# Memory of the scans reused in the tail: eight weight buffers, combination weights kept, the last two combinations side by side

## The chip, the core and the metric

The kernel runs on one core of a Trainium2 chip. Times are device microseconds of one launch, from one core. The time before is the median of three runs, 5513.0 us (5512.04 to 5520.48). The profile is one more execution, recorded by the hardware profiler.

## The reference

The input `x` holds 16 sequences of 512 rows and 256 columns. A bidirectional selective-scan layer is added to it and normalised; then follows a soft mixture of experts, with 16 experts of 64 slots each, which is added and normalised again. The last part is what the change touches:

```python
x = _layernorm(x + _L0_attn_ref(x, ...))            # scans, forward and backward
# mixture of experts, xn = layernorm(x) * g + b
logits = einsum('bnd,esd->bnes', xn, se)            # 1024 slots for each row
dispatch = softmax(logits, axis=1)                  # over the 512 rows
combine = softmax(logits.reshape(b, n, -1), -1)     # over the 1024 slots
slots = einsum('bnd,bnes->besd', xn, dispatch)
gate = gelu(einsum('besd,edf->besf', slots, Wg) + bg)
up = einsum('besd,edf->besf', slots, Wu) + bu
eout = einsum('besf,efo->beso', gate * up, Wd) + bd
y = einsum('bns,bso->bno', combine, eout)
out = _layernorm(x + y)
```

All data is float32. The experts' weights are 48 blocks of 512 KB (`Wg`, `Wu`, `Wd` for each of 16 experts).

## The kernel before

**The loop.** `seq_layers` goes through the 16 sequences. For each one it runs four scan parts (`scan_part`, two directions by two pairs of channel blocks). Beside the scans, in small pieces, it runs three streams of other work, each a list of Python generators in a `Side` object: `prep` (projections for the next scan parts), `front` (`finish`, which ends the first layer for the sequence before, and `dispatch`, which makes the slots) and `back` (`experts` and `combine` for older sequences). A generator yields how many PSUM banks its next piece needs, or `HOLD` when the results of a piece are to be taken out later. The order in which pieces are asked for sets their priority; a scheduler then places each engine's instructions, and `late` marks those that must keep their place. On each engine the instructions run strictly in the order that results from it, and so do the DMA issues of SP.

**Experts.** Sequences are taken in twos: `experts(g, 0, 8)` handles sequences 2g and 2g+1 together, 128 rows for each expert. It goes through eight pairs of experts. For a pair, PE multiplies the slots `st` with both `Wg` (L709, into `pg`), ScalarE applies gelu (L728, L731, into `ht`); then for each expert PE makes `pu` with `Wu` (L666), VectorE multiplies it into `ht` (L678), PE multiplies `ht` with `Wd` (L694, into `peo`), VectorE adds the bias `bd` (L659, into `eo`) and SP stores `eo` to `e_dram` (L660). `prefetch` (L632) keeps three weight tiles loaded or on the way, in three buffers of 512 KB. `st`, `bd` and `eo` have one buffer each: the next `bd` is loaded (L691) when `eo` has read the last one, the next `st` (L645) when the last `pu` of the pair is done.

**Combine.** `combine(b)` loads the 1024 rows of expert output of its sequence (`ceo`, L754), x1 (`cx`, L759), and for each of four blocks of 128 rows a tile of x2 (L763). For each block PE makes the logits (`cl`, L785, four matmuls of 512 columns, eight records in the profile), VectorE the maxima (L797 to L799), ScalarE exp (`cm`, L802), PE eight transposes (`ctp`, L809), ScalarE the copies (`ct`, L814), and PE eight matmuls with the expert outputs (`cpo`, L820, 16 records). The outputs carry a column of ones (L751), so `cpo` holds the sum of the weights as well: VectorE takes its reciprocal (L773) and adds the scaled result to x1 (L774). When all four blocks are done the rows are normalised (L49, L50 on VectorE; L51, L52, L488, L489 on POOL; L494 on ScalarE) and written out in one DMA (L834). `ceo` and `cx1` have one buffer, so the next combination's loads wait for this one.

**Dispatch.** For each of eight blocks of 128 slots: logits `pl` (L571), maximum (L576), exp with its sum (L579), reciprocal, scaling (L581), transposes `pd` (L585), a copy into `dis` (L590); after each second block the slots `pq` (L600), their copy `sl` (L610) and the store to `s_dram` (L619). `et`, `dis` and `sl` have one buffer.

**The tail.** After the last scan part the PSUM banks of the scans are given to a second pool (`tail`), and the rest runs without scans beside it: what is left of `combine(13)`, then `finish` and `dispatch` of sequence 15, then `experts(7, 0, 8)`, `combine(14)` and `combine(15)` in one list, one after the other (L875 to L884).

Of the kernel before, what the change touches and what calls it, by code (L numbers as in the profile page):

```python
# [9 lines left out]
F32 = mybir.dt.float32  # L10
BF16 = mybir.dt.bfloat16
AF = mybir.ActivationFunctionType
ALU = mybir.AluOpType
# [42 lines left out]
def seq_layers(tc, ident, neghalf, a, out):  # L56
# [21 lines left out]
    with ExitStack() as ctx:  # L78
# [7 lines left out]
        p2 = ctx.enter_context(tc.tile_pool(name="m_p2", bufs=2))  # L86
        p3 = ctx.enter_context(tc.tile_pool(name="m_p3", bufs=3))
        dram = ctx.enter_context(tc.tile_pool(name="m_dram", bufs=3, space=DRAM))
        ps = ctx.enter_context(tc.tile_pool(name="m_ps", bufs=3, space=PSUM))
# [5 lines left out]
        BANKS = 3  # L95
        tail = []
        count = [0]
# [162 lines left out]
        def prep_pair(b, r, p, v, gate=None):  # L260
# [18 lines left out]
            for c, q, pz in pzs:  # L279
                dts[c] = dt = p2.tile([P, L], F32, tag="dt", name=f"dt_{q}", bufs=4)  # L280
                if len(dts) == 1 and gate is None:
                    act = nc.scalar.activation(dt, pz, AF.Softplus)
                    late(act)
                else:
                    with tc.high_priority():
                        nc.scalar.activation(dt, pz, AF.Softplus)
            yield HOLD
            for c, q, pz in pzs:
                dt = dts[c]

                rr = p2.tile([P, L], F32, tag="rr", name=f"rr_{q}", bufs=4)
# [8 lines left out]
                du = p2.tile([P, L], F32, tag="du", name=f"du_{q}", bufs=4)  # L300
                nc.gpsimd.tensor_tensor(du, dt, v["u"][:, c, :], ALU.mult)
                v[c] = (dt, rr, du)
# [35 lines left out]
        def scan_part(b, r, p, v, accs, done, then):  # L338
# [4 lines left out]
            for n in range(0, NS, 2):  # L343
                q = f"{b}_{r}_{p}_{n}"

                bs = p3.tile([P, 2, L], F32, tag="bs", name=f"bs_{q}")
                cs = p3.tile([P, 2, L], F32, tag="cs", name=f"cs_{q}", bufs=2)
                for t, rows in ((bs, v["bc"][0, n : n + 2, :]), (cs, v["bc"][1, n : n + 2, :])):
                    nc.sync.dma_start(t, rows.unsqueeze(0).to_broadcast([P, 2, L]))
                for c in (2 * p, 2 * p + 1):  # L350
                    dt, rr, du = v[c]
                    db = p3.tile([P, 2, L], F32, tag="db", name=f"db_{q}_{c}")
                    nc.gpsimd.tensor_tensor(db, du.unsqueeze(1).to_broadcast([P, 2, L]), bs, ALU.mult)  # L353
                    hg = p3.tile([P, 2, L], F32, tag="hg", name=f"hg_{q}_{c}", bufs=4)
                    for j in range(2):
                        s = slice(n + j, n + j + 1)
                        h = ps_h.tile([P, L], F32, tag="h", name=f"h_{q}_{c}_{j}")
                        nc.scalar.activation(h, dt, AF.Exp, scale=w["A"][:, c, s])  # L358
                        th = p3.tile([P, L], F32, tag="th", name=f"th_{q}_{c}_{j}")
# [204 lines left out]
        def dispatch(b, xn, x2T):  # L564

            for sc in range(NSC):
# [9 lines left out]
                late(nc.vector.reduce_max(nm, pl, AX.X, negate=True))  # L576
                et = p1.tile([P, L], F32, tag="et", name=f"et_{i}")
                sm = p3.tile([P, 1], F32, tag="sm", name=f"sm_{i}")
# [42 lines left out]
        def experts(g, lo, hi):  # L621
# [10 lines left out]
            def prefetch():  # L632
                while len(got) < min(used[0] + 3, len(needs)):
                    key, e = needs[len(got)]
                    t = p2.tile([P, 4 * DM], F32, tag="W", name=f"{key}_{g}_{e}", bufs=3)
                    src = a[key][e]
# [109 lines left out]

        def combine(b):


            eo = p1.tile([P, NSC, DM + 1], F32, tag="ceo", name=f"ceo_{b}")  # L750
            nc.gpsimd.memset(eo[:, :, DM : DM + 1], 1.0)  # L751
            own = e_dram[:, b * SL : (b + 1) * SL, :]
            for j in range(2):
# [3 lines left out]
                )  # L757
            x1 = p1.tile([P, NL, DM], F32, tag="cx1", name=f"cx1_{b}")
            nc.sync.dma_start(x1, x1_dram[b].rearrange("(c p) d -> p c d", p=P))  # L759

            def load_x2(lc):
                t = p2.tile([P, NM, P], F32, tag="cx2", name=f"cx2_{b}_{lc}")
                nc.sync.dma_start(t, x2_dram[b, :, :, lc * P : (lc + 1) * P].rearrange("k p l -> p k l"))  # L763
                return t

            x2 = load_x2(0)
            yield 0
            prev = []

            def take_in():  # L770
                lc, po = prev.pop()
                sm = p3.tile([P, 1], F32, tag="csm", name=f"csm_{b}_{lc}")
                late(nc.vector.reciprocal(sm, po[:, DM : DM + 1]))  # L773
                nc.vector.scalar_tensor_tensor(  # L774
                    x1[:, lc, :], po[:, :DM], sm, x1[:, lc, :], ALU.mult, ALU.add
                )

            for lc in range(NL):
                i = f"{b}_{lc}"
                yield 2  # L780
                cls = []
                for h in range(2):
                    cl = bank(f"cl_{i}_{h}")
                    for k in range(NM):
                        nc.tensor.matmul(  # L785
                            cl,
                            x2[:, k, :],
                            seT[:, k, h * 512 : (h + 1) * 512],
                            start=(k == 0),
                            stop=(k == NM - 1),  # L790
                        )
                    cls.append(cl)
                if lc + 1 < NL:
                    x2 = load_x2(lc + 1)
                yield HOLD
                nm = p3.tile([P, 3], F32, tag="cnm", name=f"cnm_{i}")
                late(nc.vector.reduce_max(nm[:, 0:1], cls[0], AX.X))  # L797
                nc.vector.reduce_max(nm[:, 1:2], cls[1], AX.X)
                nc.vector.reduce_max(nm[:, 2:3], nm[:, 0:2], AX.X, negate=True)  # L799
                cms = [p3.tile([P, 512], F32, tag="cm", name=f"cm_{i}_{h}") for h in range(2)]  # L800
                for cm, cl in zip(cms, cls):
                    nc.scalar.activation(cm, cl, AF.Exp, bias=nm[:, 2:3])  # L802
                yield 2
                pts = []
                for h in range(NSC // 4):
                    pt = bank(f"ctp_{i}_{h}")
                    for j in range(4):
                        s = slice(j * P, (j + 1) * P)
                        nc.tensor.transpose(pt[:, s], cms[h][:, s], ident)  # L809
                    pts.append(pt)  # L810
                yield HOLD
                cts = [p3.tile([P, 512], F32, tag="cm", name=f"ct_{i}_{h}") for h in range(2)]
                for h, pt in enumerate(pts):
                    ins = nc.scalar.copy(cts[h], pt)  # L814
                    if h == 0:
                        late(ins)
                yield 1
                po = bank(f"cpo_{i}")
                for sc in range(NSC):
# [6 lines left out]
                    )  # L826
                prev.append((lc, po))
                yield HOLD
                take_in()
            mv, rs = row_stats(nc, p2, x1, neghalf, "c1")  # L830
            sh = shifts(mv, rs, "c1")
            yield 0
            scaled(x1, x1, sh, rs)
            nc.scalar.dma_start(out[b].rearrange("(c p) d -> p c d", p=P), x1)  # L834

# [40 lines left out]
        scan_psum.close()  # L876
        tail.append(ctx.enter_context(tc.tile_pool(name="t_ps", bufs=5, space=PSUM)))
        BANKS = 8
        back.drain()
        front.drain()  # L880
        g = nb // 2 - 1
        for gen in (experts(g, 0, 8), combine(2 * g), combine(2 * g + 1)):
            back.add(1, gen)
        back.drain()  # L884

# [45 lines left out]
```

## Time and profile before

| what | value |
|---|---|
| median of three runs | 5513.0 us |
| the profiled execution | 5517.41 us |
| its span, first to last instruction | 5515.6 us |
| mean granted TensorE clock | 0.861 |
| busy: PE, VectorE, ScalarE, POOL | 4004.2, 4522.2, 4097.3, 4998.6 us |
| last scan transpose on PE | ends at 5189.9 us |
| last dispatch matmul (`pq`) of sequence 15 | ends at 5298.1 us |
| last `eo` of the experts | ends at 5414.4 us |
| first `cpo` of `combine(14)` | starts at 5423.2 us |

Busy time is the time in which an engine ran an instruction. The slices of the page divide the span into 40 equal parts, with one digit for the busy tenths of each. A row of the stretches gives the same by engine for a chosen window. A wait names the engine and line that waited, what ended the wait, and the total, the number and the longest. The chain of work is followed back from the last instruction, at each step to what released it.

### The profile page before, as it was taken

Reading aid. Unit: us, or ns where it says so; the run is one execution under the profiler, and the core shown is the slowest. Engines: PE = TensorE matmul, PEld = TensorE weight load, DVE = VectorE, ACT = ScalarE, POOL = GpSimd, SP = SyncE. Lnnn points to the kernel's source line nnn. Section 1 sums busy time; section 2 is a strip of 40 time slices with the busy share of each in tenths; the row PEclk is TensorE's granted clock in tenths of the full one; section 3 lists DMA queues with packets and bytes.
Section 4 is the critical chain, followed back from the end, with each engine's and each line's share of the span. In section 5 each row is a group of like instructions: output and inputs, shape, how many; then the busy total and the mean of one; then the engine's idle time right before and its main releaser. Section 6 shows DMA issues by size and latency. Waiting matters only on the chain.

```text
span 5515.6 us, 67752 instructions
## 1 busy us (share of the span) xinstructions
PE 4004.2 (73%) x21330; PEld 3097.9 (56%) x21330; DVE 4522.2 (82%) x6210; ACT 4097.3 (74%) x6662; POOL 4998.6 (91%) x2525
## 2 busy tenths in 40 slices
PE   4556656777777777777777777777777777877777
PEld 3434444666556655666555655566556556566565
DVE  7787878888888889889888888888898898888512
ACT  6667677778778887878878787788778788777522
POOL 6999999999999999999999999999999999989500
PEclk7667777888988989888998899989899889999998
DMA  4333333565445654465545654456544665467253
GB/s 132 112 108 126 121 117 124 167 199 188 157 138 195 203 193 140 144 207 193 172 139 173 203 191 151 147 190 203 186 144 146 203 195 172 137 212 240 83 161 96
DMA packets 493852, 897.76 MB, mean 163 GB/s; under 512 B 44307, under 2 KB 291731, under 8 KB 493493
## 3 DMA queue, kind: packets, MB, share of 16 engines
q1 hardware_dynamic: 454836, 851.48, 47.6%
q10 hardware_dynamic: 38656, 41.95, 2.2%
q8 instruction: 169, 2.77, 0.2%
q14 instruction: 191, 1.56, 0.1%
HBM read 832.47 MB, written 60.82 MB: 162 GB/s over the span
## 4 chain that ended last, share of the span: by engine, by line
DVE 34%; ACT 24%; PE 18%; issue 11%; POOL 10%; DMA 3%; SPq 0%; DVEq 0%; ACTq 0%; POOLq 0%
DVE h L364 9%; DVE h L362 9%; DVE hg L367 8%; ACT h L358 5%; ACT th L360 5%; POOL hg L368 4%; POOL db L353 4%; PE acc L317 3%; PE px L244 2%; DVE rr L299 2%; PE cl L785 2%; PE pg L709 2%; ACT L358 2%; PE cpo L820 1%; ACT ht L731 1%
## 5 line engine op out<-in xcount | busy, mean ns | idle before, releaser
L353 POOL TENSOR_TENSOR db<-du,bs 128x1024 f32<-128x1024 f32 x1024 | 2431.3, 2374 | 113.8 <-DVE h L362 48.6
L368 POOL TENSOR_TENSOR hg<-hg,cs 128x1024 f32<-128x1024 f32 x1024 | 2427.6, 2371 | 25.4 <-DVE hg L367 17.6
L367 DVE SCALAR_TENSOR_TENSOR hg<-th,h 128x512 f32<-128x512 f32 x2048 | 1352.3, 680 | 251.1 <-ACT th L360 139.9
L317 PE MATMUL acc<-ident,hg 128*128 128x128 f32 x8192 | 1214.9, 301 | 391.4 <-POOL hg L368 316.0
L317 PEld LDWEIGHTS acc<-ident,hg 128*128 128x128 f32 x8192 | 1069.2, 157 | 634.1 <-POOL hg L368 410.9
L364 DVE TENSOR_TENSOR_SCAN h<-h,db 128x512 f32<-128x512 f32 x1024 | 1227.2, 1221 | 191.0 <-ACT h L358 155.2
L362 DVE TENSOR_TENSOR_SCAN h<-h,db 128x512 f32<-128x512 f32 x1024 | 1222.8, 1221 | 180.6 <-ACT h L358 131.7
L358 ACT ACTIVATE h<-dt,A_f 128x512 f32<-128x512 f32 x1024 | 699.9, 683 | 319.2 <-DVE hg L367 316.5
L358 ACT ACTIVATE h<-dt,A_b 128x512 f32<-128x512 f32 x1024 | 700.0, 684 | 292.6 <-DVE hg L367 290.9
L360 ACT ACTIVATE th<-rr,Ah_b 128x512 f32<-128x512 f32 x1024 | 728.0, 711 | 0.3
L360 ACT ACTIVATE th<-rr,Ah_f 128x512 f32<-128x512 f32 x1024 | 726.9, 710 | 0.2
L694 PE MATMUL peo<-Wd,ht 128*128 128x256 f32 x1024 | 314.8, 461 | 190.4 <-DVE ht L678 129.4
L694 PEld LDWEIGHTS peo<-Wd,ht 128*128 128x128 f32 x1024 | 223.2, 227 | 263.1 <-DVE ht L678 143.3
L709 PE MATMUL pg<-st,Wg 128*128 128x128 f32 x2048 | 277.7, 297 | 85.5 <-ACT xb L219 40.6
L785 PE MATMUL cl<-seT,cx 128*128 128x512 f32 x512 | 279.4, 689 | 75.3 <-DVE rr L299 36.7
L709 PEld LDWEIGHTS pg<-st,Wg 128*128 128x128 f32 x2048 | 265.7, 211 | 97.2 <-ACT xb L219 42.1
L666 PE MATMUL pu<-st,Wu 128*128 128x128 f32 x2048 | 270.2, 288 | 33.3 <-ACT ht L731 11.8
L666 PEld LDWEIGHTS pu<-st,Wu 128*128 128x128 f32 x2048 | 257.5, 203 | 57.0 <-ACT ht L731 16.8
L571 PE MATMUL pl<-x2T,seT 128*128 128x512 f32 x512 | 261.1, 634 | 22.9 <-DVE xf L168 12.5
L600 PE MATMUL pq<-dis,xn 128*128 128x256 f32 x1024 | 253.8, 405 | 15.7 <-ACT dis L590 13.0
L820 PE MATMUL cpo<-ceo,ct 128*128 128x257 f32 x1024 | 249.3, 398 | 21.9 <-ACT ct L814 17.0
L751 POOL MEMSET ceo<- 128x8 f32 x16 | 2.0, 124 | 260.4 <-PE cpo L820 259.4
(146 smaller groups left out, 5356.6 us busy)
## 6 DMA issues: line engine op xcount, KB each, us to landing
bs<-bc SPq DMA_DIRECT2D x512, 512.0 KB, 4.6
cs<-bc SPq DMA_DIRECT2D x512, 512.0 KB, 3.7
Wg<-in_Wg_dram SPq DMA_DIRECT2D x128, 512.0 KB, 5.4
Wu<-in_Wu_dram SPq DMA_DIRECT2D x128, 512.0 KB, 5.7
Wd<-in_Wd_dram SPq DMA_DIRECT2D x128, 512.0 KB, 5.6
bd<-in_bd_dram SPq DMA_DIRECT2D x128, 128.0 KB, 4.7
s_dram<-sl ACTq DMA_DIRECT2D x64, 256.0 KB, 2.9
st<-s_dram SPq DMA_DIRECT2D x128, 128.0 KB, 4.3
```

Source lines behind the costliest of these rows:

```text
L317: ins = nc.tensor.matmul(accs[c][:, s], hc[:, j, s], ident, is_transpose=True, start=False, stop=(last and j == 1 and lc == NL - 1),)
L353: nc.gpsimd.tensor_tensor(db, du.unsqueeze(1).to_broadcast([P, 2, L]), bs, ALU.mult)
L358: nc.scalar.activation(h, dt, AF.Exp, scale=w["A"][:, c, s])
L360: nc.scalar.activation(th, rr, AF.Tanh, bias=LN_1E12 / 2, scale=w["Ah"][:, c, s])
L362: nc.vector.tensor_tensor_scan(h, h, db[:, j, :], 0.0, ALU.mult, ALU.add)
L364: nc.vector.tensor_tensor_scan(h[:, ::-1], h[:, ::-1], db[:, j, ::-1], 0.0, ALU.mult, ALU.add)
L367: nc.vector.scalar_tensor_tensor(hg[:, j, :], th, 1.0, h, ALU.add, ALU.mult)
L368: nc.gpsimd.tensor_tensor(hg, hg, cs, ALU.mult)
L666: nc.tensor.matmul(pu[:, fc * P : (fc + 1) * P], got["Wu", e][:, k, fc * P : (fc + 1) * P], st[:, k, :, j * SL : (j + 1) * SL], start=(k = ...
L694: nc.tensor.matmul(po[:, :DM], ht[:, fc, :], got["Wd", e][:, fc, :], start=(fc == 0), stop=(fc == NF - 1))
L709: nc.tensor.matmul(pg[:, fc * P : (fc + 1) * P], got["Wg", e][:, k, fc * P : (fc + 1) * P], st[:, k, :, j * SL : (j + 1) * SL], start=(k = ...
L785: nc.tensor.matmul(cl, x2[:, k, :], seT[:, k, h * 512 : (h + 1) * 512], start=(k == 0), stop=(k == NM - 1),)
```

## The change

The pools of the scans' SBUF tiles are put into one pool, `m_scan` (`p4`), which is closed after the last scan part. A new pool, `t_sb`, takes its memory (`wide`). While `wide` is set:

- the experts' weights have eight buffers in place of three (`AHEAD`), and `prefetch` asks for eight;
- `dispatch` has three `et` buffers in place of one;
- the weights of a combination (logits, exp, transposes, copies) are a generator of their own, `weights`, and `all_weights` runs it for the four blocks of a sequence and keeps the eight copied tiles;
- `combine` takes kept tiles if it is given them, and then does only `cpo`, the sum, the norm and a write for each block of 128 rows (128 KB each) in place of one norm and one write at the end;
- `ceo` of sequence 15 has its own buffer; both x1 tiles are in the buffers of `x`; the column of ones is set by VectorE in place of POOL.

The tail then runs two lists in turn, a piece of each: the rest of `combine(13)` and `all_weights(14)` beside `finish` and `dispatch` of sequence 15; the experts beside `all_weights(15)`; `combine(14)` beside `combine(15)`.

```diff
+        scan_room = ctx.enter_context(ExitStack())
+        p4 = scan_room.enter_context(tc.tile_pool(name="m_scan", bufs=3))
...
-                dts[c] = dt = p2.tile([P, L], F32, tag="dt", name=f"dt_{q}", bufs=4)
+                dts[c] = dt = p4.tile([P, L], F32, tag="dt", name=f"dt_{q}", bufs=4)
...
-                et = p1.tile([P, L], F32, tag="et", name=f"et_{i}")
+                if wide:
+                    et = wide[0].tile([P, L], F32, tag="tet", name=f"et_{i}", bufs=3)
+                else:
+                    et = p1.tile([P, L], F32, tag="et", name=f"et_{i}")
...
-                while len(got) < min(used[0] + 3, len(needs)):
+                while len(got) < min(used[0] + (AHEAD if wide else 3), len(needs)):
                     key, e = needs[len(got)]
-                    t = p2.tile([P, 4 * DM], F32, tag="W", name=f"{key}_{g}_{e}", bufs=3)
+                    if wide:
+                        t = wide[0].tile([P, 4 * DM], F32, tag="tW", name=f"{key}_{g}_{e}", bufs=AHEAD)
+                    else:
+                        t = p2.tile([P, 4 * DM], F32, tag="W", name=f"{key}_{g}_{e}", bufs=3)
...
+        def weights(b, lc, x2, keep):
...
+            cts = []
+            for h, pt in enumerate(pts):
+                if keep:
+                    ct = wide[0].tile([P, 512], F32, tag="tct", name=f"ct_{i}_{h}", bufs=4 * NL)
+                else:
+                    ct = p3.tile([P, 512], F32, tag="cm", name=f"ct_{i}_{h}")
+                ins = nc.scalar.copy(ct, pt)
...
+        def all_weights(b, kept):
+            x2 = [load_x2(b, 0)]
+            yield 0
+            for lc in range(NL):
+                kept[b, lc] = yield from weights(b, lc, x2, True)
+
+        def combine(b, kept=None):
+            eo = (wide[0] if wide and b % 2 else p1).tile([P, NSC, DM + 1], F32, tag="ceo", name=f"ceo_{b}")
+            (nc.vector if wide else nc.gpsimd).memset(eo[:, :, DM : DM + 1], 1.0)
...
+            if wide:
+                x1 = p2.tile([P, NL, DM], F32, tag="x", name=f"cx1_{b}")
...
+                cts = kept.pop((b, lc)) if kept else (yield from weights(b, lc, x2, False))
...
+                if kept is not None:
+                    put(lc, lc + 1, *norm(lc, lc + 1))
+            if kept is None:
+                stats = norm(0, NL)
+                yield 0
+                put(0, NL, *stats)
...
+        scan_room.close()
+        wide.append(ctx.enter_context(tc.tile_pool(name="t_sb", bufs=1)))
         BANKS = 8
-        back.drain()
-        front.drain()
-        g = nb // 2 - 1
-        for gen in (experts(g, 0, 8), combine(2 * g), combine(2 * g + 1)):
-            back.add(1, gen)
-        back.drain()
+        def side_by_side():
+            while front.gens or back.gens:
+                for x in sides:
+                    x.take_up()
+                for x in (front, back):
+                    x.piece()
+
+        g, kept = nb // 2 - 1, {}
+        back.add(1, all_weights(2 * g, kept))
+        side_by_side()
+        front.add(1, experts(g, 0, 8))
+        back.add(1, all_weights(2 * g + 1, kept))
+        side_by_side()
+        front.add(1, combine(2 * g, kept))
+        back.add(1, combine(2 * g + 1, kept))
+        side_by_side()
```

More of the change, by code (lines that the diff above doesn't have):

```diff
@@ L95, in seq_layers @@
         BANKS = 3
-        tail = []
+        AHEAD = 8
+        tail, wide = [], []
         count = [0]
@@ L289, in prep_pair @@
                 dt = dts[c]
-                rr = p2.tile([P, L], F32, tag="rr", name=f"rr_{q}", bufs=4)
+                rr = p4.tile([P, L], F32, tag="rr", name=f"rr_{q}", bufs=4)
                 if r == 0:
@@ L299, in prep_pair @@
                 late(nc.vector.tensor_tensor_scan(o, ins[0], ins[1], 0.0, ALU.add, ALU.max))
-                du = p2.tile([P, L], F32, tag="du", name=f"du_{q}", bufs=4)
+                du = p4.tile([P, L], F32, tag="du", name=f"du_{q}", bufs=4)
                 nc.gpsimd.tensor_tensor(du, dt, v["u"][:, c, :], ALU.mult)
@@ L344, in scan_part @@
                 q = f"{b}_{r}_{p}_{n}"
-                bs = p3.tile([P, 2, L], F32, tag="bs", name=f"bs_{q}")
-                cs = p3.tile([P, 2, L], F32, tag="cs", name=f"cs_{q}", bufs=2)
+                bs = p4.tile([P, 2, L], F32, tag="bs", name=f"bs_{q}")
+                cs = p4.tile([P, 2, L], F32, tag="cs", name=f"cs_{q}", bufs=2)
                 for t, rows in ((bs, v["bc"][0, n : n + 2, :]), (cs, v["bc"][1, n : n + 2, :])):
@@ L351, in scan_part @@
                     dt, rr, du = v[c]
-                    db = p3.tile([P, 2, L], F32, tag="db", name=f"db_{q}_{c}")
+                    db = p4.tile([P, 2, L], F32, tag="db", name=f"db_{q}_{c}")
                     nc.gpsimd.tensor_tensor(db, du.unsqueeze(1).to_broadcast([P, 2, L]), bs, ALU.mult)
-                    hg = p3.tile([P, 2, L], F32, tag="hg", name=f"hg_{q}_{c}", bufs=4)
+                    hg = p4.tile([P, 2, L], F32, tag="hg", name=f"hg_{q}_{c}", bufs=4)
                     for j in range(2):
@@ L358, in scan_part @@
                         nc.scalar.activation(h, dt, AF.Exp, scale=w["A"][:, c, s])
-                        th = p3.tile([P, L], F32, tag="th", name=f"th_{q}_{c}_{j}")
+                        th = p4.tile([P, L], F32, tag="th", name=f"th_{q}_{c}_{j}")
                         nc.scalar.activation(th, rr, AF.Tanh, bias=LN_1E12 / 2, scale=w["Ah"][:, c, s])
@@ L745, in experts, with load_x2 @@
                     take_out()
-        def combine(b):
-            eo = p1.tile([P, NSC, DM + 1], F32, tag="ceo", name=f"ceo_{b}")
-            nc.gpsimd.memset(eo[:, :, DM : DM + 1], 1.0)
+        def load_x2(b, lc):
+            t = p2.tile([P, NM, P], F32, tag="cx2", name=f"cx2_{b}_{lc}")
+            nc.sync.dma_start(t, x2_dram[b, :, :, lc * P : (lc + 1) * P].rearrange("k p l -> p k l"))
+            return t
+        def weights(b, lc, x2, keep):
+            i = f"{b}_{lc}"
+            yield 2
+            t = x2.pop()
+            cls = []
+            for h in range(2):
+                cl = bank(f"cl_{i}_{h}")
+                for k in range(NM):
+                    nc.tensor.matmul(
+                        cl, t[:, k, :], seT[:, k, h * 512 : (h + 1) * 512], start=(k == 0), stop=(k == NM - 1)
+                    )
+                cls.append(cl)
+            if lc + 1 < NL:
+                x2.append(load_x2(b, lc + 1))
+            yield HOLD
+            nm = p3.tile([P, 3], F32, tag="cnm", name=f"cnm_{i}")
+            late(nc.vector.reduce_max(nm[:, 0:1], cls[0], AX.X))
+            nc.vector.reduce_max(nm[:, 1:2], cls[1], AX.X)
+            nc.vector.reduce_max(nm[:, 2:3], nm[:, 0:2], AX.X, negate=True)
+            cms = [p3.tile([P, 512], F32, tag="cm", name=f"cm_{i}_{h}") for h in range(2)]
+            for cm, cl in zip(cms, cls):
+                nc.scalar.activation(cm, cl, AF.Exp, bias=nm[:, 2:3])
+            yield 2
+            pts = []
+            for h in range(NSC // 4):
+                pt = bank(f"ctp_{i}_{h}")
+                for j in range(4):
+                    s = slice(j * P, (j + 1) * P)
+                    nc.tensor.transpose(pt[:, s], cms[h][:, s], ident)
+                pts.append(pt)
+            yield HOLD
+            cts = []
[5 more added lines that the diff above has]
+                ins = nc.scalar.copy(ct, pt)
+                if h == 0:
+                    late(ins)
+                cts.append(ct)
+            return cts
@@ L757, in combine @@
                 )
-            x1 = p1.tile([P, NL, DM], F32, tag="cx1", name=f"cx1_{b}")
+            if wide:
+                x1 = p2.tile([P, NL, DM], F32, tag="x", name=f"cx1_{b}")
+            else:
+                x1 = p1.tile([P, NL, DM], F32, tag="cx1", name=f"cx1_{b}")
             nc.sync.dma_start(x1, x1_dram[b].rearrange("(c p) d -> p c d", p=P))
[L761 to L764, printed above, removed]
@@ L766, in combine @@
-            x2 = load_x2(0)
-            yield 0
[L768 to L776, printed above, removed]
+            x2 = [] if kept else [load_x2(b, 0)]
+            yield 0
@@ L778, in combine, with norm, put @@
+            def norm(lo, hi):
+                mv, rs = row_stats(nc, p2, x1[:, lo:hi, :], neghalf, f"c{hi - lo}")
+                return shifts(mv, rs, f"c{hi - lo}"), rs
+            def put(lo, hi, sh, rs):
+                scaled(x1[:, lo:hi, :], x1[:, lo:hi, :], sh, rs)
+                nc.scalar.dma_start(out[b].rearrange("(c p) d -> p c d", p=P)[:, lo:hi, :], x1[:, lo:hi, :])
             for lc in range(NL):
                 i = f"{b}_{lc}"
-                yield 2
-                cls = []
@@ L782, in combine @@
[L782 to L816, printed above, removed]
+                cts = kept.pop((b, lc)) if kept else (yield from weights(b, lc, x2, False))
@@ L826, in combine @@
                     )
-                prev.append((lc, po))
                 yield HOLD
[L829 to L834, printed above, removed]
+                sm = p3.tile([P, 1], F32, tag="csm", name=f"csm_{i}")
+                late(nc.vector.reciprocal(sm, po[:, DM : DM + 1]))
+                nc.vector.scalar_tensor_tensor(x1[:, lc, :], po[:, :DM], sm, x1[:, lc, :], ALU.mult, ALU.add)
+                if kept is not None:
[4 more added lines that the diff above has]
+                put(0, NL, *stats)
         FINISH, COMBINE, PAIR = 30, 13, 5
```

## The prediction

> **What bounds the kernel now.** I read the profile from the end backwards, because the diff touches only what follows the last scan. The page first: its slices (138 us each) and the span.
>
> ```profile
> span 5515.6 us, 67752 instructions
> ...
> DVE  7787878888888889889888888888898898888512
> ACT  6667677778778887878878787788778788777522
> POOL 6999999999999999999999999999999999989500
> ```
>
> POOL, VectorE and ScalarE, which bound the scans, are nearly idle in the last two slices: a tail of some 326 us follows other laws. Next the stretches of that tail (columns: stretch, its length, PE, PE weight loads, VectorE, ScalarE, POOL busy with counts, granted clock, DMA share, GB/s):
>
> ```profile
> 5186.00:5216.00 30.00, 21.57 (x98) 14.77 (x96) 6.98 (x16) 7.96 (x14) 1.82 (x5) 0.97 0.06 18
> ...
> 5253.00:5266.00 13.00, 9.78 (x31) 6.77 (x30) 0.85 (x2) 3.58 (x7) 0.00 (x0) 0.74 0.13 40
> ...
> 5337.00:5352.00 15.00, 12.27 (x84) 10.78 (x82) 3.01 (x10) 2.28 (x8) 0.00 (x0) 1.00 0.85 262
> ...
> 5430.00:5463.00 33.00, 29.18 (x103) 18.10 (x103) 8.57 (x23) 7.30 (x12) 0.11 (x1) 0.95 0.04 13
> 5463.00:5516.00 53.00, 33.67 (x122) 21.87 (x120) 11.69 (x31) 13.76 (x24) 3.41 (x8) 0.86 0.22 55
> ```
>
> The timeline gives the borders. (A) 5189.9 (last scan transpose) to 5298.1 (last pq): rest of combine(13), finish and dispatch of sequence 15, 108.2 us; a chain of short hand-overs in which PE idles and its clock falls (0.74), DMA at 0.06 to 0.13. (B) to 5414.4 (last eo): the experts of the last two sequences, 116.3 us, DMA share 0.85, PE busy 12.3 of 15. (C) to 5515.6: the two combinations one after the other, 101.2 us. Together 325.7.
>
> Last, what B waits for (the waits between 5307 and 5412: us, times, longest) and one pair of it in the chain of work:
>
> ```profile
> DVE eo L659 <- DMA bd<-in_bd_dram: 47.9, 10, 5.9
> ...
> PE peo L694 <- DVE ht L678: 11.6, 12, 2.7
> PE pg L709 <- DMA st<-s_dram: 4.0, 7, 1.5
> PE pu L666 <- DMA Wu<-in_Wu_dram: 2.7, 2, 1.6
> PE pg L709 <- DMA Wg<-in_Wg_dram: 2.6, 4, 0.9
> ```
> ```profile
> 5358.67 1.80 PE pu L666 x16
> 5360.48 0.37 SPq L639
> 5360.94 4.07 DMA bd<-in_bd_dram
> 5365.20 0.28 issue
> 5365.48 0.35 DVE ht L678
> ```
>
> PE waits 5.3 us for weights (Wu, Wg) over seven pairs, but 11.6 for ht. ht of the second expert stands on VectorE behind eo of the first, and that waits for bd, which has one buffer and stands on SP behind a weight load that pu releases. Weights are only a part of what holds a pair.
>
> **The change part by part.** The sum is made against the profiled span; its own run took 5517.4 us, 1.8 more, and the median of the three runs is 5513.0. I subtract the difference from the median. In the built program the order of all engines up to the last scan instruction is the same, but for one 512 KB load of x1 (sequence 14) on SP, moved into the scan of sequence 15 behind a wait for ScalarE's last xn; that ends at 4946.4, and SP comes there at 4948.4. So no stall, and the scans cost 0.
>
> *Removed from C.* Per 128 rows, a combination has on PE cl 3.6, transposes 1.23, cpo 3.7 (from 5448.4 to 5452.1), and waits for max, exp and copies; eight of these leave only cpo. C becomes: last eo to first cpo was 8.8 us (store landing 3.3, ceo load 5.1, both still alone on the path); four ceo loads instead of two share the queues, I add 1.0 (0 to 2): 9.8. Then eight cpo of alternating sequences. The first is cold: 6.8 at 5423.2, after 5 us of idle PE. Seven more at 3.7 are 25.9. The rest of a row block per cpo is VectorE 0.17+0.48+0.43+0.18, POOL 1.7, ScalarE 0.5: less than 3.7 each, hidden behind the next cpo. After the last one: VectorE 1.5, POOL 2.2, ScalarE 0.7 with one block instead of four, issue and landing 3.1 (a 512 KB write took 3.6): 7.5 against 9.7. C = 9.8+6.8+25.9+7.5 = 50.0, a gain of 51.2.
>
> Here a rule weighs against the row: the Trainium skill, "TensorE: Matmul & The Clock Gate" (Part 1: The HAM clock gate), says that an idle array runs at half clock for about the first 3.4 us of work. That makes an estimate of 1.7 us extra for the first cpo; the row shows 3.1 (6.8 against 3.7). I take the row; by the rule C is 1.4 shorter.
>
> *Moved into A: weights of sequence 14.* 4 x (3.6+1.23) = 19.3 us of PE. The order now alternates combine(13) and finish(15): two rounds of pyt 1.0, cl 3.6, wait for exp about 1.6, ctp 1.2, po 3.7, cpo 3.7 = 14.9, so 29.8 with the second po ending at 25.8. From po to the norm's scaling 4.0, x 2.1; ScalarE then has cx of sequence 13 before the last three xn (its POOL chain ends 3.5 after cpo): xn is complete at 37.4. One and a half cl (5.4) fill that. Transposes, two exps, x2T and the next cl: first pl at 41.8, where it was 47.0. The first dispatch pair took 16.9; with the remaining cl 7.2 and ctp 3.7 in its waits the hand-overs (pl to pd 4.4, behind cm on VectorE and ScalarE) make 21.7. The next two pairs have nothing between and gain nothing from three et buffers, since the generator asks for pl, pd, pl, pd, pq in turn: 17.25 each (5266.5 to 5283.8, pq cold at 6.2 instead of 3.7). Before, the first of them took 12.7 because one pl stood ahead. Fourth pair 14.3, with cl in place of pu: 14.6. A = 41.8+21.7+34.5+14.6 = 112.6, a loss of 4.4. Bounds: minus 6 (both pq warm, the first pair no longer than before) to plus 14 (19.3 exposed, less the 5.2 of the interleaved start).
>
> *Eight weight buffers.* Their memory is free only after the scans, so the three loads that went out early go with five more at 5190: 8 x 0.52 MB at 262/0.85 = 308 GB/s, 13.6 us, needed 100 us later. Without that cover they would cost those 13.6. The pairs: PE needs pg 3.9, pu 2x1.95, peo 2x2.0 = 11.8. In the new order bd is still on SP behind a load that waits for pu of the same pair, and st, bd, eo have one buffer as before. So from pg: 3.9+2.0, then SP 0.9, bd 4.2 to 4.5, eo 0.4, ht 0.4, peo 2.0, and the next pg: 13.9, with 0.8 of hand-overs 14.7, against 15.4 (92.5 us for six pairs). The Wg and Wu waits go, what is late next is bd. Six pairs: 88.1. Below, 12.5 if bd came early (11.8 and one wait for ht 0.7); above, 15.4. I take 14.7, the nearest rows.
>
> *Moved into B: weights of sequence 15.* Into the first two pairs go three cl (10.8; one lies in A) and four transposes (4.9). PE work there: 21.8+15.7 = 37.5. Waits: about 1.0 for the third Exp, 0.8 of small ones, then st after the last pu (4.2, of which peo covers 2.4): 41.1 against 23.8. B = 41.1+88.1 = 129.2, a loss of 12.9 (0 with pairs at 12.5, 17 with pairs at 15.4).
>
> ScalarE now changes its table five times in B instead of twice. A rule speaks against the change: "ScalarE: Activation LUTs" (Table sets: the hidden batching unit) says to batch calls by set, at some 2.7 us a switch with its drain. The row: load at 5299.54, first gelu at 5300.84, 1.3 us. Two of the three extra ones run while PE does cl or ctp, one is in the 1.0 above. By the rule's price I would add 3 x 1.4 = 4.2; with the row 0.
>
> *Small ones:* memset on VectorE instead of POOL (0.1) and x1 in its own buffer (in the chain from 5468.9 a write of 3.8 and a load of 3.8 stood in C, which the 50.0 no longer has).
>
> Sum: +4.4 +12.9 -51.2 = -33.9; 5513.0 - 33.9 = **5479 us**.
>
> **The rivals.** (1) *Weights are what held the pairs*: then pairs 2 to 7 run at 12.5, 13 us less: 5466. For it DMA share 0.85; against it the bd row. (2) *The moved work is not hidden*: 38.6 us of PE is paid in full instead of 17.3: 5500, and with the table switches at the page's price 5504. For it, ScalarE and VectorE take the streams in a fixed order, so each waits for the other's slowest; against it, PE is idle a quarter of A. (3) *Slower*: eight loads stand in the SP queue ahead of st and bd, which then land late in every pair. One load is 1.7 us at 308 GB/s; four ahead make 6.8, eight pairs 54: 5533. It decides from 33.9/8 = 4.2 us a pair, two and a half loads. For it, all share SP's queue; against it, a load is released every 2 us by one consumed tile, and st stands ahead of the next Wg. (4) *It doesn't do what it says*: waits on shared memory keep the old order in time; 5513. The built order speaks against it.
>
> **How the numbers follow.** Likeliest 0.60 (5479, its own range 5468 to 5492), (1) 0.14, (2) 0.17, (3) 0.05, (4) 0.04. The range leaves out (3), (4) and the outer ends of (1) and (2): 5464 to 5500. The measurement tells 0.2% (11 us) from no change: faster 0.91, same 0.04, slower 0.05.
>
> **What would show it.** From last scan transpose to last pq about 113 us, to last eo 129, to the end 50; eight cpo in a row, the first near 6.8; pairs 2 to 7 at 14.7 with eo still waiting for bd; Wu and Wg waits gone; five table loads in B. Wrong would be: pairs near 12.5 or above 16, a dispatch pair longer than 18, or cpo with waits between.

## The result, and the profile after

The changed kernel takes 5469.4 us (median; 5463.0 to 5474.8). The kernel before has a median of 5516.0 us in four runs, the three of the first section and one more, so the ratio is 0.9915 (95% interval 0.9898 to 0.9932), 46.6 us less. The prediction was 5479 us with a range of 5464 to 5500: right in sign, inside its range and some 10 us too slow.

The profiled execution of the changed kernel took 5474.8 us, span 5473.0. Its scans end at 5195.0 us, 5.1 later than in the profile of before, with the same instructions in the same order. In all profiles of this study they end between 5189 and 5199 us, so I compare stages and not only whole times. The three stages of the tail, in a view of windows (start and end of the stretch, its length, busy PE, PE weight loads, VectorE, ScalarE, POOL with counts, granted clock, DMA share, GB/s), first of before, then of after:

```profile
5189.90:5298.10 108.20, 75.83 (x282) 51.53 (x282) 16.35 (x41) 33.94 (x65) 5.10 (x13) 0.86 0.13 44
5298.10:5414.40 116.30, 92.55 (x614) 80.64 (x613) 24.93 (x81) 21.72 (x68) 0.00 (x0) 1.00 0.81 247
5414.40:5515.60 101.20, 72.14 (x251) 46.48 (x250) 21.14 (x56) 23.49 (x40) 3.52 (x9) 0.86 0.18 45
```

```profile
5195.00:5301.90 106.90, 88.59 (x339) 56.74 (x337) 24.07 (x58) 43.40 (x82) 4.96 (x12) 0.94 0.27 85
5301.90:5428.10 126.20, 106.81 (x681) 92.96 (x679) 28.97 (x89) 33.51 (x85) 0.00 (x0) 0.95 0.69 213
5428.10:5473.00 44.90, 29.74 (x128) 25.39 (x128) 10.09 (x32) 4.80 (x8) 9.71 (x32) 0.86 0.30 69
```

The last stage lost 42.4 us of PE work (72.14 to 29.74) and 56.3 us of length. The first took 12.8 us more of PE work and is 1.3 shorter; the experts took 14.3 more and are 9.9 longer. The tail went from 325.7 to 278.0 us.

What the experts wait for in their pairs 2 to 7 (waits of after; us, times, longest):

```profile
DVE eo L668 <- DMA bd<-in_bd_dram: 40.8, 9, 5.7
...
PE peo L703 <- DVE ht L687: 14.4, 10, 4.0
```

The waits for Wu, Wg and st that stood here before are gone, and the bd wait of eo is still there. One pair in the chain of work of after:

```profile
5371.01 1.80 PE pu L675 x16
...
5372.94 0.50 SPq L648
...
5373.53 6.08 DMA bd<-in_bd_dram
...
5380.03 0.35 DVE ht L687
5380.38 0.04 issue
5380.43 3.78 PE peo L703 x8
5384.21 4.26 PE pg L718 x32
```

It is the chain of before with other numbers: bd goes out on SP behind a weight load (L648) that had to wait for pu. The landing of bd, 4.4 us in the median of before, is 5.4 in the median here and 6.1 in this pair. In this pair PE idles for 4.0 us ahead of peo, the granted clock is 0.84 from 5367 to 5384, and peo takes 3.78 in place of 1.99, pg 4.26 in place of 3.57. A wait of 2.85 us two blocks of peo later left peo at 2.00.

The end of the same chain, from the last eo on:

```profile
5428.09 2.81 DMA e_dram<-eo
...
5430.96 5.62 DMA ceo<-e_dram
...
5436.72 29.76 PE cpo L844 x128
```

Eight combinations stand in one row, with no wait between them.

### The profile page after: what moved, and what is told of

Its sections match the earlier page's. It is cut to its first block, busy times and chain, and to the rows that moved or that the text cites. A ratio compares the mean times of both kernels' runs of the same rounds, so it can differ in the third digit from the quotient of the medians.

```text
span 5473.0 us, 67758 instructions
## 1 busy us (share of the span) xinstructions
PE 4001.2 (73%) x21317; PEld 3106.7 (57%) x21330; DVE 4522.5 (83%) x6212; ACT 4101.0 (75%) x6665; POOL 5003.5 (91%) x2547
## 4 chain that ended last, share of the span: by engine, by line
DVE 33%; ACT 24%; PE 19%; issue 11%; POOL 10%; DMA 3%; SPq 0%; DVEq 0%; ACTq 0%; POOLq 0%
DVE h L367 9%; DVE h L365 8%; DVE hg L370 8%; ACT h L361 5%; ACT th L363 5%; POOL db L356 4%; POOL hg L371 4%; PE acc L320 3%; PE px L247 2%; PE pg L718 2%; DVE rr L302 2%; PE cl L770 2%; ACT L361 2%; PE peo L703 2%; ACT ht L740 1%
## 5 line engine op out<-in xcount | busy, mean ns | idle before, releaser
L770 PE MATMUL cl<-seT,cx 128*128 128x512 f32 x512 | 275.7, 681 | 74.0 <-DVE rr L302 35.7
L675 PEld LDWEIGHTS pu<-st,Wu 128*128 128x128 f32 x2048 | 256.5, 202 | 52.5 <-ACT ht L740 13.2
L574 PE MATMUL pl<-x2T,seT 128*128 128x512 f32 x512 | 260.0, 632 | 24.3 <-DVE xf L171 14.6
L606 PE MATMUL pq<-dis,xn 128*128 128x256 f32 x1024 | 254.6, 406 | 15.4 <-ACT dis L596 12.7
L606 PEld LDWEIGHTS pq<-dis,xn 128*128 128x128 f32 x1024 | 206.3, 207 | 49.8 <-ACT dis L596 15.6
```

The lines of the kernel that those rows point to most:

```text
L606: nc.tensor.matmul(pq[:, k * 256 : (k + 1) * 256], xn[:, lc, k * P : (k + 1) * P], dis[:, lc, :], start=(lc == 0), stop=(lc == NL - 1),)
L675: nc.tensor.matmul(pu[:, fc * P : (fc + 1) * P], got["Wu", e][:, k, fc * P : (fc + 1) * P], st[:, k, :, j * SL : (j + 1) * SL], start=(k = ...
```

## The experiments

The table gives the median, the ratio to the kernel before on the same chip, and the stages of each profile: A from the last scan transpose to the last pq; B in two parts, its first two expert pairs and the other six, split where the pg block of pair 2 begins; C from the last eo to the end. In b3, c0, c1 and d0 the order of PE puts 8 to 10 of the 32 pg records of pair 2 ahead of that block, and these count with the first part. Measured from block to block the result is the same: in c1 the pg blocks of pairs 3 and 7 start 46.6 us apart, 11.7 a pair.

| kernel | us | ratio (95%) | A | B, pairs 0-1 | B, pairs 2-7 (each) | C |
|---|---|---|---|---|---|---|
| before | 5516.0 | | 108.2 | 23.8 | 92.5 (15.4) | 101.2 |
| after | 5469.4 | 0.9915 (0.9898-0.9932) | 106.9 | 35.8 | 90.4 (15.1) | 44.9 |
| a0, after again | 5467.5 | 0.9910 (0.9896-0.9925) | 107.0 | 35.7 | 87.4 (14.6) | 44.7 |
| a1, 3 weight buffers | 5477.6 | 0.9929 (0.9914-0.9944) | 108.1 | 35.7 | 92.6 (15.4) | 45.5 |
| a2, 3 bd buffers | 5469.0 | 0.9912 (0.9896-0.9929) | 106.9 | 35.7 | 89.5 (14.9) | 45.2 |
| a3, both | 5473.7 | 0.9923 (0.9908-0.9938) | 108.0 | 35.8 | 91.8 (15.3) | 45.8 |
| b0, memory alone | 5508.3 | 0.9980 (0.9972-0.9987) | 109.8 | 22.9 | 86.8 (14.5) | 96.1 |
| b1, side by side alone | 5481.0 | 0.9930 (0.9915-0.9945) | 98.1 | 22.5 | 90.7 (15.1) | 77.9 |
| b2, weights of 15 early | 5455.6 | 0.9882 (0.9867-0.9897) | 107.5 | 23.2 | 85.2 (14.2) | 45.0 |
| b3, st, eo, bd buffers | 5472.4 | 0.9912 (0.9898-0.9927) | 108.4 | 36.5 | 84.2 (14.0) | 46.0 |
| c0, small loads out | 5455.2 | 0.9877 (0.9860-0.9893) | 107.3 | 36.5 | 71.5 (11.9) | 45.1 |
| c1, c0 with b2 | 5443.9 | 0.9858 (0.9843-0.9873) | 108.6 | 22.0 | 70.4 (11.7) | 46.1 |
| d0, c1 with ceo in parts | 5431.9 | 0.9830 (0.9814-0.9847) | 110.6 | 22.0 | 70.4 (11.7) | 34.4 |

### Unchanged, on the same chip

> The changed kernel as it is, to compare the next three with on the same chip: 5469 us (5463 to 5475); last scan transpose to last pq 107 us, to last eo 126, to the end 45; pairs 2 to 7 of the experts 15.1 us each.

5467.5 us. One program gives pairs of 14.6 us in one profile and 15.1 in another, so half a microsecond a pair says nothing by itself.

### Three weight buffers

```diff
-        AHEAD = 8
+        AHEAD = 3
```

> Three weight buffers in the tail in place of eight, all else as changed. Theory (bd, not the weights, holds a pair): pairs 2 to 7 stay at 15.1 to 15.4 us with Wg and Wu waits back in place of a part of the bd wait, total within 4 us of 5469. Rival 1 (the eight buffers carry a gain): pairs at 17 or more, total 5480 or more. Rival 3 in its small form (the deep prefetch delays bd): bd lands in 4.5 us again in place of 5.4, pairs at 14.4, total 5465.

5477.6 us, 10 above a0. The theory's number (within 4 us) missed, and the intervals of the two ratios still overlap. Pairs 2 to 7 are 5.2 us longer than in a0 and 2.2 longer than in the other profile of the same kernel, after. In the profile PE waits again for st (3.9 us), Wg (0.9), Wu (0.8) and Wd (0.6), while eo waits 34.9 us for bd and not 40.8: two limits take turns. bd lands in 4.7 us, against 5.0 (a0) and 5.4 (after) with eight buffers, so the small form of rival 3 is there, but the pairs with eight buffers are still the shorter ones. The medians give the eight buffers 8 to 10 us (against after and a0), the pairs of the profiles 2 to 5: a gain is likely, its size is not settled.

### bd asked for early

```diff
-                bd = p2.tile([P, DM], F32, tag="bd", name=f"bd_{g}_{e}", bufs=1)
+                if wide:
+                    bd = p2.tile([P, 4 * DM], F32, tag="W", name=f"bd_{g}_{e}", bufs=3)[:, :DM]
+                else:
+                    bd = p2.tile([P, DM], F32, tag="bd", name=f"bd_{g}_{e}", bufs=1)
```

> Eight weight buffers, and in the tail three bd buffers in place of one, so that bd is asked for two or three experts ahead. Theory: the wait of eo for bd (41 us in pairs 2 to 7) goes, what is late next is st or the weights, pairs at 12.5 to 13.5 us, total 5455 to 5460. Rival (the DMA engines, 0.81 to 0.85 busy, are what holds a pair): pairs stay at 15, total 5469, with Wg, Wu or st waits in place of the bd wait.

5469.0 us, no gain: the theory's pairs of 12.5 to 13.5 did not come. But the rival's waits for Wg and Wu did not come either. The chain of work of a2:

```profile
5347.08 1.80 PE pu L675 x16
5348.88 0.02 issue
5348.89 4.83 DMA st<-s_dram
5353.73 0.14 issue
5353.86 0.68 PE pg L721 x4
```

bd is off the chain, and st has taken its place at once. The waits of a2 in its pairs 2 to 7 have no bd; they have st, and VectorE now waits for the store of eo, which has one buffer too:

```profile
DVE eo L668 <- DMA e_dram<-eo: 14.1, 4, 3.8
PE pg L721 <- DMA st<-s_dram: 12.2, 5, 2.9
```

The load of st may start when the last pu of the pair is done, in the chain it takes 3.9 to 5.3 us, and pg of the next pair needs it. That loop is 9 to 10 us from pg to the last pu and 4 to 5 for st: 14 to 15 again.

> Three bd buffers and three weight buffers. Theory: with bd out of the way the weights are the next limit, as three buffers stand 1.5 experts ahead: pairs 13.5 to 15 us with Wg and Wu waits, total 5460 to 5469, above the run with eight. Rival (bd was the only limit and depth is worth nothing): pairs at 12.5 to 13.5 as with eight buffers, total 5455 to 5460.

Run a3 has both edits: 5473.7 us, pairs of 15.3. It is above the run with eight buffers (5469.0), as the theory had it, and PE waits for weights (Wd 4.9 us, Wu 2.0) where a2 has no such wait. But neither run has the pairs that the theory gave it, so the two decide little.

### The parts of the change alone

Run b0 keeps the new buffers and runs the old tail; b1 adds the lists side by side, with each combination making its own weights:

```diff
+        back.drain()
+        front.drain()
+        g = nb // 2 - 1
+        for gen in (experts(g, 0, 8), combine(2 * g), combine(2 * g + 1)):
+            back.add(1, gen)
+        back.drain()
```

```diff
-        back.add(1, all_weights(2 * g, kept))
         side_by_side()
         front.add(1, experts(g, 0, 8))
-        back.add(1, all_weights(2 * g + 1, kept))
         side_by_side()
-        front.add(1, combine(2 * g, kept))
-        back.add(1, combine(2 * g + 1, kept))
+        front.add(1, combine(2 * g))
+        back.add(1, combine(2 * g + 1))
         side_by_side()
```

> The new memory alone: eight weight buffers, own ceo and x1 buffers, three et buffers, but the tail in the old order (experts, then combination of 14, then of 15, their weights made inside). Theory (the gain is in the combinations): stages 107, 115 and 94 to 98 us, total about 5510, pairs 2 to 7 of the experts at 15. Rival 1 (weights held the pairs): pairs at 12.5, total 5495. Rival 3 (the deep prefetch delays st and bd): pairs at 17 or more, total 5525.

> As b0, but the two last combinations side by side, each making its own weights (nothing kept, nothing moved into the dispatch or the experts). Theory: PE pays 2 x (3.6 + 1.2 + 3.7) for each of four pairs of blocks, 68 us, with some 10 us ahead and 9 behind: the end stage is 85 to 88 us, total about 5500, so that making the weights ahead is worth some 30 us more. Rival (most of the gain is from the side by side): end stage 65 or less, total 5480 or less.

b0 takes 5508.3 us, ratio 0.9980: the memory alone is worth some 11 us (7 to 15 by the interval), about as the theory had it; the trace has 5.1 of them in C, where ceo and x1 now have their own buffers, and 6.6 in B, against 1.6 lost in A. Its pairs 2 to 7 take 14.5 us with eight weight buffers, not the 12.5 of rival (1). b1 takes 5481.0 us, where I expected 5500. Both of its end stages are better than I reckoned. C is 77.9 and not 85 to 88, because the scheduler put the first logits of the combinations beside the last expert pair, and the rest of the first two blocks into the wait for ceo. From the timeline of PE in b1 (start, us, line, tiles, records, the idle time before):

```profile
5393.93 1.02 PE L770 MATMUL cl<-seT,cx 128*128 128x512 f32 x2
5394.96 1.99 PE L703 MATMUL peo<-Wd,ht 128*128 128x256 f32 x8
...
5401.16 5.31 PE L770 MATMUL cl<-seT,cx 128*128 128x512 f32 x12
...
5410.30 8.86 PE L844 MATMUL cpo<-ceo,ct 128*128 128x257 f32 x32 [0.90 <-ACT ct L799]
```

And A falls by 11.7 us against b0 (by 10.1 against before), where the one difference is that the rest of combine(13) alternates with finish and dispatch of sequence 15: the first pq ends 53.9 us after the scans, against 63.9 in before.

So the parts of the change are: buffers about 11 us; side by side 27 (5508.3 to 5481.0, of which A has 11.7 and C 18.2); weights made ahead 13.5 (5481.0 to 5467.5; 11 by the ratios, as the two ran on different chips). The last one saves 33.2 us in C and gives 8.9 back in A and 13.2 in the first two expert pairs. It is not the kept weights alone: `combine` normalises and writes block by block only when it is given kept weights, so b1 still does both once, at the end. From the last cpo to the end b1 takes 9.7 us and after 6.5, so some 3 of the 33 are of that.

### The weights of sequence 15 at another place

```diff
         back.add(1, all_weights(2 * g, kept))
+        back.add(1, all_weights(2 * g + 1, kept))
         side_by_side()
         front.add(1, experts(g, 0, 8))
-        back.add(1, all_weights(2 * g + 1, kept))
         side_by_side()
```

> The weights of sequence 15 are made right behind those of 14, beside its dispatch, in place of beside the first experts. Theory: PE idles in dispatch pairs 1 to 3 (23.5 us busy of 35), so the 19.3 us of PE work are hidden there (stage to last pq stays at 107 to 110), and the first two expert pairs fall from 35.8 to 25 us: total 5457 to 5462. Rival 2 (moved work is paid in full wherever it stands): stage to last pq 119, experts 12 less, total 5469.

5455.6 us, as the theory had it and 1 below its range. The first two pairs fall from 35.7 to 23.2 us, and A is 107.5 for 107.0: the same 19 us of PE work cost 13 beside the experts and next to nothing beside the dispatch. Windows of dispatch, first of after (its second and third pair), then of b2 (the end of its second pair to the last pq):

```profile
5253.00:5288.00 35.00, 23.47 (x70) 14.95 (x69) 3.42 (x8) 11.23 (x23) 0.00 (x0) 0.80 0.07 23
```

```profile
5264.00:5297.00 33.00, 29.41 (x136) 19.86 (x135) 6.50 (x14) 15.45 (x31) 0.00 (x0) 1.00 0.15 48
```

In after PE idles a third of that stretch at a granted clock of 0.80; in b2 it is busy nine tenths of it at 1.00. A pq block takes 3.70 us in b2 where after has two of 6.2, so the moved work pays a part of itself by keeping PE at speed. First a pq of after, then of b2:

```profile
5281.52 6.18 PE L606 MATMUL pq<-dis,xn 128*128 128x256 f32 x16 [0.68 <-ACT dis L596]
```

```profile
5278.80 3.70 PE L606 MATMUL pq<-dis,xn 128*128 128x256 f32 x16
```

### All small loads out of the way

Run b3 gives st and eo two buffers and asks for st a pair ahead (six weight buffers make room); bd as in a2. Run c0 does the same, but loads bd for four experts at once into a freed weight buffer, before the experts begin:

```diff
+                    st = wide[0].tile([P, NM, 2, 2 * SL], F32, tag="tst", name=f"st_{g}_{ep}", bufs=2)
...
+                    eo = wide[0].tile([P, DM], F32, tag="teo", name=f"eo_{g}_{e}", bufs=2)
...
                 used[0] += 2
+                now = st
+                if wide and ep + 1 < hi:
+                    st = load_slots(ep + 1)
```

```diff
+            def load_bias(c):
+                t = p2.tile([P, 4 * DM], F32, tag="W", name=f"bd4_{g}_{c}", bufs=3)
+                t = t.rearrange("p (e d) -> p e d", e=4)
+                nc.sync.dma_start(t, a["bd"][4 * c : 4 * c + 4, :].unsqueeze(0).to_broadcast([P, 4, DM]))
+                four[c] = t
...
+                    bd = four[e // 4][:, e % 4, :]
```

> As the run with three bd buffers, but st asked for one pair ahead in two buffers and eo in two buffers (six weight buffers, to make room). With bd early the next pg waited 3.9 to 5.2 us for st from the last pu on. Theory (bd, st and eo, small loads each in one buffer, hold a pair in turn): without all three PE is busy to the end of the pair, 12 to 12.8 us each, total 5452 to 5458. Rival (the DMA engines hold a pair; 3.1 MB of weights at the 300 GB/s seen are 10.5 us and the rest waits in the queue): pairs at 14 to 15, total 5464 to 5469, with Wg, Wu and Wd waits.

5472.4 us, no gain over a0. The weight waits of the rival did not come, and the bd wait of the theory did not go:

```profile
DVE eo L674 <- DMA bd<-in_bd_dram: 29.8, 6, 8.4
```

With six weight buffers the order of SP has bd, three buffers or not, behind a weight load that waits for pu of the same pair; in the chain it then lands 4.6 to 7.3 us later. A free buffer doesn't make a load early; its place in the queue does. b3 therefore decides nothing about the DMA engines.

> The small loads of a pair taken out of the way for good: bd for four experts in one load into the freed weight buffers (asked for before the experts begin, the fourth in pair 3), st one pair ahead in two buffers, eo in two buffers, six weight buffers. In run b3 bd was still asked for behind a weight load (bd wait 29.8 us in six pairs), so it did not decide. Theory (small loads behind weight loads in one queue, each with few buffers, hold a pair): no bd and no st wait, pairs 12 to 12.8 us, total 5452 to 5458. Rival (the DMA engines hold a pair): pairs stay at 14 to 15 with waits for Wg, Wu and Wd, total 5464 to 5472.

> c0 with the weights of sequence 15 made beside its dispatch as in b2. Theory: both gains add, first two pairs 12 to 13 each as well: 5456 less 15: total 5438 to 5445. Rival (DMA holds a pair): as b2, 5453 to 5458.

c0 takes 5455.2 us and c1, with the weights as in b2, 5443.9: both as the theory had it. The pairs take 11.9 and 11.7 us. All three small loads went out of the way at once here; no run tells what st and eo are worth apart. A pair of c1 in the timeline of PE:

```profile
5357.39 3.73 PE L740 MATMUL pg<-st,Wg 128*128 128x128 f32 x32
5360.96 1.95 PE L692 MATMUL pu<-st,Wu 128*128 128x128 f32 x16
5363.42 1.99 PE L725 MATMUL peo<-Wd,ht 128*128 128x256 f32 x8 [0.51 <-DVE ht L704]
5365.25 1.95 PE L692 MATMUL pu<-st,Wu 128*128 128x128 f32 x16
5367.04 0.83 PE L740 MATMUL pg<-st,Wg 128*128 128x128 f32 x6
5367.71 1.99 PE L725 MATMUL peo<-Wd,ht 128*128 128x256 f32 x8
5369.54 3.06 PE L740 MATMUL pg<-st,Wg 128*128 128x128 f32 x26
```

PE waits for nothing but half a microsecond of ht. The stretch around this pair:

```profile
5350.00:5365.00 15.00, 13.97 (x100) 12.99 (x100) 4.23 (x14) 3.10 (x12) 0.00 (x0) 1.00 1.01 340
```

The DMA engines carry 340 GB/s here, and 328 and 305 in the stretches of 15 us on either side, so in before, at 247 and a share of 0.81, they were not what held a pair at 15. But they are at their end now as PE is: a share of 0.9 to 1.0, and in c0 one load of Wu stands on the chain,

```profile
5361.24 1.80 PE pu L692 x16
5363.04 0.02 issue
5363.06 7.28 DMA Wu<-in_Wu_dram
```

ahead of a stretch (5365 to 5380) with a DMA share of 1.00.

### Expert outputs in two parts

```diff
-            for j in range(2):
-                nc.sync.dma_start(
-                    eo[j * SL : (j + 1) * SL, :, :DM],
-                    own.rearrange("(c j) s o -> j s c o", j=2)[j],
-                )
+            for lo, hi in ((0, NSC - 1), (NSC - 1, NSC)) if kept is not None else ((0, NSC),):
+                for j in range(2):
+                    nc.sync.dma_start(
+                        eo[j * SL : (j + 1) * SL, lo:hi, :DM],
+                        own.rearrange("(c j) s o -> j s c o", j=2)[j][:, lo:hi],
+                    )
```

> c1 with each load of the expert outputs (ceo) cut in two: 14 experts as soon as these are stored, the last two behind. Theory (the 9 us from the last eo to the first cpo are a store of 2.8 and a load of 5.6 in a row, with nothing beside them): the store stays, the last load is an eighth of the size and lands in 3 to 4, and PE has up to 5 us of cpo work before it: end stage 45 to 39 or 41, total 5438 to 5441. Rival (the early part finds the queues full of the last weights, or PE turns cold as before): no change, 5444.

5431.9 us, more gain than expected: 12 less than c1, and 85 to 103 us less than before (ratio 0.9814 to 0.9847). C is 34.4 us, where 39 to 41 were expected. The timeline of PE around the last expert:

```profile
5394.51 1.99 PE L725 MATMUL peo<-Wd,ht 128*128 128x256 f32 x8 [0.51 <-DVE ht L704]
5396.34 6.25 PE L870 MATMUL cpo<-ceo,ct 128*128 128x257 f32 x28
5402.99 21.98 PE L870 MATMUL cpo<-ceo,ct 128*128 128x257 f32 x100 [0.40 <-DMA ceo<-e_dram]
```

28 of the 128 records run while the last two experts' outputs are stored and loaded, and of 9 us of idle PE 0.4 are left. The first cpo is no longer slow either (6.25 us for 28 records, where the first 16 of c1 took 6.7), which the expectation had not counted.

## Why the prediction was right, and where it was off

**The sum.** Predicted -33.9 us for the tail, measured -47.7 in the profiles (325.7 to 278.0). All three stages were shorter than predicted: A 106.9 for 112.6, B 126.2 for 129.2, C 44.9 for 50.0. The errors all point one way, so the sum was not helped by errors that cancel, except inside B (5.3 too long in pairs 0 and 1, 2.3 too short in pairs 2 to 7). The 5.1 us that the scans took longer in the profile of after are the scatter of one execution; the medians differ by 46.6 us.

The total alone could not have told the theory from rival (1): 5469.4 lies nearer to the rival's 5466 than to 5479. The pairs decide. Rival (1) needs 12.5 us each; after has 15.1, and eo still waits for bd.

**C, 50.0.** Right in kind: eight cpo in a row, cl, maxima, exp and transposes gone. Last eo to first cpo 8.6 (predicted 9.8: of the 1.0 added for the sharing of four ceo loads 0.5 was paid, 5.62 for 5.14, and the store of eo took 2.81 for 3.32), the eight cpo 29.7 (32.7), the end 6.5 (7.5). Of the 3.0 in the middle, about half is the first cpo, 5.4 us where 6.8 was taken: 1.75 more than one of the later ones, not 3.1. The granted clock shows why. First the windows of before from its first cpo on, then of after:

```profile
5423.00:5427.00 4.00, 3.78 (x9) 3.07 (x10) 0.00 (x0) 0.00 (x0) 0.00 (x0) 0.50 0.00 0
5427.00:5431.00 4.00, 4.00 (x11) 2.79 (x11) 0.90 (x3) 0.00 (x0) 0.00 (x0) 0.70 0.00 0
```

```profile
5436.70:5441.00 4.30, 4.28 (x12) 3.54 (x13) 0.00 (x0) 0.00 (x0) 0.00 (x0) 0.60 0.30 50
5441.00:5466.00 25.00, 25.00 (x117) 21.77 (x116) 8.83 (x28) 3.60 (x6) 8.45 (x28) 1.00 0.10 32
```

The records of the clock in these traces are all 0.50 or 1.00. So the first cpo of before ran at half clock for 6.2 us (3.8 of the first window, 2.4 of the second) and that of after for 3.4 (0.60 over 4.3 us); half of each is 3.1 and 1.7, the extra times.

I had weighed the row's 3.1 extra against an estimate of 1.7 from the Trainium skill, "TensorE: Matmul & The Clock Gate" (Part 1: The HAM clock gate), and taken the row. That the rule was nearer this time is chance: in c1 PE idles for the same 9 us ahead of the first cpo, the clock stays at 0.50 for the first 4.0 us and at 0.73 over the next 4, and the extra is 3.1 again; in a0, the same program as after, it is 1.5.

**A single mis-sized term: the length of a block against its pitch.** The other half of those 3.0, and 2.3 of the 5.3 by which pairs 0 and 1 were over-estimated (41.1, measured 35.8), have one cause. I added block lengths from rows where PE waited before and after each block, where the pitch, from the start of one block to the start of the next, was needed. When work is queued, the next block starts before the last one ends: in the timeline of c1 a pu block of 1.95 is followed after 1.78 or 1.79, and in after a cpo of 3.64 comes every 3.5 (seven of them take 24.5 us). In pairs 0 and 1 of after the blocks add up to 36.5 us by their rows and occupy 34.2. The blocks were also 1.0 shorter than the 37.5 reckoned, and of my 3.6 us of waits there 1.75 remained (ctp for exp 1.31, peo for ht 0.44).

**A, 112.6.** The term that was mis-sized is the interleaved start. I gave it 5.2 us (first pl at 41.8 with half a cl in its gaps, and then a first pair longer by 4.8); b1 shows it alone, 10.0 us by the end of the first pq. With the moved weights the first pl came at 38.8 and the first pair took 18.6 instead of 21.7: 6.1 us together, more than the whole error of A. The later pairs were as predicted (35.3 for 34.5, 14.2 for 14.6), the missing use of the three et buffers included: no pair is shorter for them. That PE had room in pairs 1 to 3, the prediction saw (pq at a low clock), and b2 shows that it could be used.

**B, pairs 2 to 7, 14.7 each.** Right: 14.6 and 15.1 in two profiles, Wg and Wu waits gone, bd still on the chain. Its reason is half right. bd was on the chain, but not alone: the lower bound "12.5 if bd came early", on which rival (1)'s 5466 rested as well, is false by itself. a2 took bd away and st held the pair at 14.9, so the number 14.7 came out right without testing the reason: the loop of st is as long as that of bd. With bd, st and eo all early a pair takes 11.7 (c1). I had st in the list of single buffers and in the first two pairs' waits (4.2 us, covered by 2.4 of peo), and did not follow it once bd was gone.

**Weights moved into B.** Predicted 17.3 for the two first pairs, measured 12.0 against before: the pitch above, and the waits that did not come. The ScalarE table loads, five of them as predicted, cost what the row said: all of PE's waits for exp in those pairs are 1.3 us, and one switch between exp and gelu (5321.85 to 5323.16) took 1.3 us from end to start. By the price of "ScalarE: Activation LUTs" (Table sets: the hidden batching unit) they would have cost 4.2 more.

**The rivals.** (1) fell in its form: with three buffers and no other edit pairs 2 to 7 lose 2 to 5 us, not 13, and with eight they do not reach 12.5. (2) fell: moved work was paid by about half (22.1 of 38.6, a0 against b1). (3) is there in miniature: bd lands in 5.0 to 5.4 where before had 4.4, 0.6 to 1.0 us a load, where rival (3) needed 4.2 a pair; pairs 2 to 7 are no longer than in before all the same. (4) fell: the order in time is the built one. What stays open is how much of the difference between a1 and a0 is depth and how much scatter.

## What to carry to other kernels

When several small loads share a queue with large ones and each has one buffer, taking one of them off the chain can show the next at the same length, as bd and st did here; follow the loop of each (its last reader, its place in the queue, its landing, its first reader) before you price the removal of one, and move the request, since a spare buffer alone leaves the place in the queue as it was. Work moved off the end paid most here where it was put into a stage in which PE waits for hand-overs and has lost clock: the same 19 us cost 13 beside the experts and half a microsecond beside the dispatch. And when a total fits a rival as well as your theory, look at the stages before you believe either. When you add up blocks that will stand back to back, use their pitch in a crowded row, not their length in a waiting one.

## What the runs showed of the hardware

Three things that I had not expected. A 128x256 broadcast load, 128 KB written, took as long to land among weight loads (bd, 4.6 to 6.1 us in after) as a 512 KB weight load (Wg, 3.7 to 5.6), and somewhat longer with eight weight loads allowed ahead (medians 5.0 and 5.4) than with three (4.4 and 4.7). Work added to PE in the dispatch made its neighbours faster: pq blocks fell from 6.2 to 3.70 us as the granted clock rose from 0.80 to 1.00. And how much the first cpo is slowed does not follow from how long PE was idle: 3.1 us after 4.6 us of idle in before, 1.75 after 9.1 in after, 3.1 after 9.0 in c1. It follows how long the granted clock stays low after the first matmul, as the windows above show.
